# Moving the softmax division, the mode scalings and some loads within the rows of a shifted-window attention and Fourier block

## The chip, the core and the metric

The kernel runs on one core of a Trainium2 chip. A core has five engines, each with its own instruction list, worked off in order: TensorE (PE, matrix products; PEld is its loading of weights), VectorE (DVE), ScalarE (ACT), GpSimd (POOL) and SyncE (SP), which here only issues DMAs. The engines synchronise by semaphores. The metric is the time of one execution on the device in microseconds (us); the figure of a kernel is the median of its runs.

## The reference

The input x is 32 images of 56 x 56 positions with 128 channels, all in float32. Two residual layers follow each other:

```python
x = x + attention(_gn(x), rpb_table, w_qkv, w_proj, b_proj)
x = x + fourier(_gn(x), w0, w1, W1, b1, W2, b2)

# attention: roll by 3, windows of 7 x 7, four heads of 32 channels
qkv  = win @ w_qkv.T
attn = softmax(q * hd**-0.5 @ k.T + bias + mask)
out  = (attn @ v) @ w_proj.T + b_proj          # rolled back

# fourier: DCT along one axis, 32 modes mixed per mode, inverse DCT
x_fty = dct(x, axis=-1)                         # and the same along the other axis
out_y = einsum('bixy,ioy->boxy', x_fty[..., :32], w0)
h     = idct(out_x) + idct(out_y)
b     = relu(h @ W1 + b1) @ W2 + b2
```

`_gn` is a group normalisation over 32 groups of four channels, with mean and variance taken over a whole image.

## The kernel before

**Rows and cycles.** An image is cut into eight rows of eight windows, 256 rows in all. The main loop runs over cycles, and cycle r starts the attention of row r. One row passes through several cycles: in its own, queries and keys (`attn_qk`), scores (`attn_scores`), row maximum and its subtraction (`attn_max`: VectorE L496, GpSimd L497), exponential (`attn_exp`, ScalarE L503) and values (`attn_v`, L456, copied by ScalarE L463); in the next, the sum and its reciprocal (VectorE, L508 and L510) and the division (`attn_divide`, six GpSimd operations at L522 that also write the blocks in the form in which they are transposed); two cycles on, the transpose (`attn_transpose`, L532); three on, probabilities times values (`attn_values`, L547, evicted by ScalarE L579 and VectorE L577), the projection (`attn_project`, L592, with the residual added at L600 and stored to the DRAM tensor `scr`); four on, the sums and squares (`attn_sums`, `attn_squares`) from which the second normalisation is made.

**The Fourier layer.** It runs beside the attention of the following images, from cycle `CONV_BEGIN` = 11 on. With c counted from the cycle in which an image's Fourier part begins: c = 0 is the statistics (`fourier_stats`, a generator worked off in steps) and the transform along the width (`transform`, L699, transposed by VectorE L715 in `turn_modes`); c = 1 and 2 the transform along the height; c = 3 to 5 the mixing of the modes (`mix`, L747); c = 5 to 8 the inverse (`modes_back`, L786, fetched at L804 and L809); c = 8 to 15 without 11 the feed-forward part in seven groups (`ff_in`, `ff_out`, both by the helper `halved`, L113; the result is added at L865). Between transform and mixing, ScalarE scales the modes by the image's reciprocal deviation (`scale_modes`, L722, two operations for each half) and shifts the first mode (`shift_modes`, L727). Since c = 0 falls on the fourth row of an image, row i of the attention stands beside a fixed c: row 3 beside 0 and 8, row 5 beside 2 and 10, row 6 beside 3, row 0 beside 5 and 13.

**The next image.** It is loaded in four quarters (`load_quarter`, four DMAs each, one buffer `xin` after the first image) and transposed by VectorE (`turn_quarter`, L334 to L339); then statistics of its rows (`row_stats`, L356) and its normalisation in four steps (`image_norm`, called by `norm_step`) follow. `next_steps` says in which row each quarter and each row's statistics come.

**Order.** The order on TensorE, ScalarE, VectorE and GpSimd is the order of the program text: cycles before 11 are written out in `first_rows`, later ones are put together from `halves_first`, `eighths`, `quarters`, `behind_max` and `halves_last`. SyncE's order is left to the scheduler of the kernel's framework. A DMA that overwrites a tile waits for what wrote or read it before: `mix_weights` first sets one column of its tile with GpSimd, so that the load is not issued before GpSimd has come that far in its list.

**Buffers.** Scores lie in two buffers; up to row 8 there is a third, in `y_of[1]`, which the Fourier part uses later (`attn_buffer`). The attention takes its PSUM banks from four in rotation (`attn_bank`), the Fourier part from four others (`conv_bank`).

Of the kernel before, what the change touches and what calls it, by code (L numbers as in the profile page):

```python
# [14 lines left out]
P = 128  # L15
# [32 lines left out]
def swin_fourier_kernel(  # L48
# [212 lines left out]
    def mix_weights(k):  # L261
        dst, src = ((w1sb, w1), (w0sb, w0))[k // 4]
        m = slice(k % 4 * NM // 4, (k % 4 + 1) * NM // 4)
        nc.gpsimd.memset(dst[:, m.start, :1], 0.0)
        nc.sync.dma_start(dst[:, m], src[:, m])
# [33 lines left out]
    def attn_buffer(r):  # L299
        return a_sb[r % 3 if r < CONV_BEGIN - 2 else r % 2]  # L300
# [234 lines left out]
    def attn_values(im, i, r):  # L535
# [3 lines left out]
        po = [attn_bank(), attn_bank()]  # L539
# [104 lines left out]
    def fourier_stats(im):  # L644
        pg = attn_bank()

        for k, t in enumerate((im.tot, im.part[:, (NWR - 1) % 4])):
            t = t.rearrange("p k g -> p (k g)")
            for hs in HALVES:
                nc.tensor.matmul(  # L650
                    pg[hs, : C // 2], lhsT=gmean, rhs=t, start=(k == 0), stop=(k == 1)
                )
        own = small.tile([P, 2, C // 4], F32, tag="own", name="own", bufs=1)
        nc.vector.scalar_tensor_tensor(
            out=own,
            in0=pg[:, : C // 2].rearrange("p (k g) -> p k g", k=2),
            scalar=4.0,
            in1=gavg.unsqueeze(1).to_broadcast([P, 2, C // 4]),
            op0=ALU.mult,
            op1=ALU.mult,  # L660
        )
        ms = small.tile([P, 2], F32, tag="ms", name="ms")
        nc.vector.tensor_reduce(ms, own, axis=AX.X, op=ALU.add)
        nm2 = small.tile([P, 1], F32, tag="nm2", name="nm2")
        nc.vector.scalar_tensor_tensor(
            out=nm2, in0=ms[:, 0:1], scalar=-1.0, in1=ms[:, 0:1], op0=ALU.mult, op1=ALU.mult
        )
        ve = small.tile([P, 1], F32, tag="ve1", name="ve1")
        nc.vector.scalar_tensor_tensor(
            out=ve, in0=nm2, scalar=1e-5, in1=ms[:, 1:2], op0=ALU.add, op1=ALU.add  # L670
        )
        rstd = small.tile([P, 1], F32, tag="rstd1", name="rstd1")
        nc.gpsimd.tensor_tensor(rstd, ve, mhalf, ALU.pow)
        im.rstd = rstd
        yield
        shift = small.tile([P, 1], F32, tag="shift", name="shift")
        nc.vector.scalar_tensor_tensor(
            out=shift, in0=ms[:, 0:1], scalar=-SQRT_S, in1=rstd, op0=ALU.mult, op1=ALU.mult
        )
        im.shift = shift  # L680
        yield
# [36 lines left out]
    def scale_modes(im, width, h):  # L718

        y = y_of[width][:, : NM * S].rearrange("p (k h n r) -> p h r n k", k=NM, h=2, r=2)[:, h]  # L720
        for r, t in enumerate(im.modes.pop((width, h))):
            nc.scalar.mul(y[:, r], t.rearrange("p (n k) -> p n k", k=NM), im.rstd)  # L722
# [226 lines left out]
    def halves_first(cycle):  # L949
        begins = [im for im, c in fourier(cycle) if c == 0]  # L950
        last, j = row(cycle - 4)
        tokens_bias(cycle)
        divide(cycle)
# [11 lines left out]
        if cycle % NWR == 0:  # L965
            norm_step(cycle)
        if cycle % NWR == NWR - 1:
            norm_step(cycle)
# [23 lines left out]
    def half_columns(cycle, rest=False):  # L992
        for im, c in fourier(cycle):
            if rest and c != 3:
                continue
            if c == 0:
                next(im.stats, None)
            elif c == 3:
# [22 lines left out]
    def eighths(cycle):  # L1021
# [3 lines left out]
        for im, c in fourier(cycle):  # L1025
            if c == 0:
                for h in range(2):
                    transform(im, True, h)
                    turn_modes(im, True, h)
            if c in (1, 2):  # L1030
# [15 lines left out]
    def first_scale(cycle):  # L1046
        for im, c in fourier(cycle):
            if c == 0:
                shift_modes(im, True)
            elif c in (1, 2):  # L1050
                scale_modes(im, False, c - 1)
                if c == 2:
                    shift_modes(im, False)

    def width_scale(cycle):
        for im, c in fourier(cycle):
            if c == 0:
                for h in range(2):
                    scale_modes(im, True, h)
# [9 lines left out]
    def next_steps(cycle):  # L1069
        b, i = divmod(cycle, NWR)  # L1070
        steps = {
            int(b == 0): ((0, 0), ()),
            1 + int(b == 0): ((0, 1), ()),
            4: ((1, 0), (0, 1, 2)),
            5: ((1, 1), (3, 4, 5)),
            6: (None, (6, 7)),
        }
        return (b + 1, *steps.get(i, (None, ()))) if b + 1 < NB else (b + 1, None, ())

    def next_quarter(cycle):  # L1080
        b, quarter, _ = next_steps(cycle)
        if quarter:
            turn_quarter(images[b], *quarter)

    def wrap_rows(cycle):
        b, _, _ = next_steps(cycle)
# [3 lines left out]
    def next_groups(cycle):  # L1090
        b, _, rows = next_steps(cycle)
# [7 lines left out]

    def halves_last(cycle):  # L1100
# [3 lines left out]
        width_scale(cycle)  # L1104
# [9 lines left out]
        first_scale(cycle)  # L1114
# [5 lines left out]
    def next_begin(cycle):  # L1120
        b, quarter, _ = next_steps(cycle + 1)
# [7 lines left out]
    def first_rows(cycle):  # L1129
        im, i = row(cycle)  # L1130
        im3, i3 = row(cycle - 3)
        if im:
            attn_qk(im, i)
        if cycle:
# [4 lines left out]
        if im:  # L1139
            attn_scores(im, i, cycle)  # L1140
            attn_max(cycle)
        divide(cycle)
# [3 lines left out]
        for _ in range(cycle in (0, NWR - 1, NWR)):  # L1146
            norm_step(cycle)
        last, j = row(cycle - 4)
        if last:
            attn_sums(last, j)  # L1150
            attn_squares(last, j)
            add_sums(last, j)
# [7 lines left out]
        next_quarter(cycle)  # L1160
# [18 lines left out]
    with tc.manual_schedule(engines={ET.PE, ET.Activation, ET.DVE, ET.Pool}):  # L1179
# [13 lines left out]
        extra = y_of[1][:, : NH * NP * WT].rearrange("p (t w j) -> p t w j", t=NH, w=NP)  # L1193
        a_sb.append(extra)
        for cycle in range(NB * NWR + CONV_BEGIN + FF_AT[-1] - NWR + 1):
# [4 lines left out]
            if not row(cycle - 3)[0]:  # L1200
# [3 lines left out]
                width_scale(cycle)  # L1204
                half_columns(cycle)
                half_columns(cycle, True)
                first_scale(cycle)
# [79 lines left out]
```

## Time and profile before

| | us |
|---|---|
| median of three runs | 3293.78 |
| lowest and highest run | 3292.73, 3294.27 |
| the profiled execution, its own time | 3297.98 |
| its span, first to last instruction | 3296.2 |
| mean granted TensorE clock (share of full speed) | 0.991 |
| VectorE, ScalarE, GpSimd busy | 2605.2, 2057.4, 2335.7 |
| largest group on GpSimd: division L522, 1518 operations | 1289.4 |
| largest group on ScalarE: L830, 896 operations | 499.4 |
| idle of GpSimd before L522, waiting for the reciprocal L510 | 263.0 |

The profile is of one execution. An operation is named by its line, its engine and its tiles, output first: `y<-modes,rstd` writes y from modes and rstd. An idle time is put down to what ended it last, as `<-ENGINE tile line`. Engines other than the limiting one may idle at no cost. Times within the span are counted from its first instruction. TensorE's matmuls overlap, so that two of them in a row start closer together than one lasts.

### The profile page before, as it was taken

The page shows a single profiled execution, that of the slowest core. Times are in us where ns is not written, and L with a number is a line of the kernel's source. Part 1 is how long each engine was busy: PE and PEld are TensorE (multiplying, and loading weights), DVE is VectorE, ACT ScalarE, POOL GpSimd, SP SyncE. Part 2 cuts the span into 40 slices and gives each one's busy share as a digit, 9 for nine tenths or more (in the row PEclk, how much of TensorE's full clock was granted, in tenths as well). Part 3 has the DMA queues.
Part 4 walks back from the last instruction along what each step waited for, and adds up shares of the span by engine and source line. Part 5 has one row for each costly group of instructions (what it writes and reads, how often), then busy time and mean ns, then how long its engine had stood idle before and what let it go on. Part 6 is the DMA issues. An engine that isn't in the chain of part 4 may idle for free.

```text
span 3296.2 us, 151336 instructions
## 1 busy us (share of the span) xinstructions
PE 3170.4 (96%) x65408; PEld 2394.9 (73%) x65408; DVE 2605.2 (79%) x5098; ACT 2057.4 (62%) x3680; POOL 2335.7 (71%) x2610
## 2 busy tenths in 40 slices
PE   4689999999999999999999999999999999999999
PEld 3467777777777777777777777777777777777776
DVE  7888888887888878888888888877888887888751
ACT  3456666666666666666666666666666666666663
POOL 7777777777777777777777777777777777777741
PEclk9799999999999999999999999999999999999999
DMA  6555555555555555555555555555555655555453
GB/s 105 116 124 142 140 138 142 133 146 140 137 140 135 136 145 138 138 142 138 139 144 143 136 142 138 136 142 143 137 139 136 143 139 139 138 143 135 121 140 96
DMA packets 1168160, 448.40 MB, mean 136 GB/s; under 512 B 520107, under 2 KB 1137629, under 8 KB 1167493
## 3 DMA queue, kind: packets, MB, share of 16 engines
q1 hardware_dynamic: 1159300, 437.38, 54.9%
q8 instruction: 514, 8.42, 1.1%
q10 hardware_dynamic: 7584, 1.18, 0.3%
q14 instruction: 154, 1.25, 0.1%
q0 software_dynamic: 608, 0.17, 0.0%
HBM read 276.97 MB, written 161.48 MB: 133 GB/s over the span
## 4 chain that ended last, share of the span: by engine, by line
PE 76%; ACT 10%; DVE 7%; POOL 3%; DMA 2%; issue 2%; SPq 1%; ACTq 0%; POOLq 0%; DVEq 0%
PE pc L113 35%; PE pa L113 9%; PE pa L456 7%; PE pc L747 5%; PE pc L786 5%; PE pa L592 5%; PE pa L478 4%; PE pa L547 4%; ACT k L443 2%; PE pc L699 2%; ACT hid L830 2%; ACT y L722 2%; POOL a L497 2%; DVE modes L715 1%; DVE a L486 1%
## 5 line engine op out<-in xcount | busy, mean ns | idle before, releaser
L522 POOL TENSOR_TENSOR blocks<-a,rs 128x512 f32<-128x512 f32 x1518 | 1289.4, 856 | 483.9 <-DVE rs L510 263.0
L113 PE MATMUL pc<-wff,hid 128*64 128x128 f32 x12544 | 742.0, 273 | 1.3 <-ACT hid L830 1.0
L113 PE MATMUL pc<-xf,wff 128*64 128x512 f32 (+2 forms) x3584 | 718.9, 539 | 1.1 <-DVE xf L804 0.9
L113 PEld LDWEIGHTS pc<-wff,hid 128*64 128x64 f32 x12544 | 706.5, 137 | 11.1 <-ACT hid L830 5.3
L497 POOL TENSOR_TENSOR a<-a,mx 128x784 f32<-128x784 f32 x253 | 381.4, 1508 | 314.9 <-DVE mx L496 281.6
L113 PEld LDWEIGHTS pc<-xf,wff 128*64 128x64 f32 x3584 | 280.6, 136 | 354.9 <-issue 239.9
L830 ACT ACTIVATE hid<-pc,b1sb 128x512 f32<-128x512 f32 (+2 forms) x896 | 499.4, 643 | 42.7 <-PE pc L113 42.7
L463 ACT COPY v<-pa 128x512 f32<-128x512 f32 x256 | 151.9, 593 | 482.8 <-PE pa L456 482.7
L113 PE MATMUL pa<-xw,wn 128*64 128x392 f32 x2048 | 400.4, 501 | 31.3 <-ACT wn L412 28.8
L865 DVE TENSOR_TENSOR res<-pc,res 128x512 f32<-128x512 f32 (+3 forms) x257 | 142.9, 567 | 319.4 <-issue 173.2
L503 ACT ACTIVATE a<-a 128x784 f32<-128x784 f32 x253 | 217.3, 859 | 281.4 <-POOL a L497 281.4
L486 DVE TENSOR_TENSOR a<-pa,bm 128x392 f32<-128x392 f32 x506 | 261.1, 557 | 84.8 <-PE pa L478 70.6
L837 POOL TENSOR_TENSOR res<-res,b2sb 128x512 f32<-128x512 f32 (+2 forms) x256 | 265.3, 1042 | 87.4 <-DMA res<-scr 78.4
L443 ACT ACTIVATE k<-pa,bqkv,heads 128x392 f32<-128x392 f32 x512 | 318.1, 673 | 8.0 <-PE pa L113 0.9
L532 DVE STREAM_TRANSPOSE eT<-blocks 128x1024 f32<-128x1024 f32 x256 | 313.6, 1225 | 2.4 <-POOL blocks L522 2.4
L127 POOL TENSOR_TENSOR xr<-xr,bproj 128x384 f32<-128x384 f32 (+1 forms) x256 | 292.8, 1144 | 25.6 <-DMA xr<-in_x_dram 17.1
L456 PE MATMUL pa<-wn,xw 128*64 128x128 f32 x4096 | 289.5, 283 | 8.6 <-issue 2.5
L547 PEld LDWEIGHTS pa<-eT,v 49*32 49x32 f32 x16384 | 173.6, 106 | 154.3 <-ACT hid L830 48.7
L592 PE MATMUL pa<-wproj,oT 128*64 128x128 f32 x3584 | 251.8, 276 | 19.6 <-DVE oT L577 17.4
L508 DVE TENSOR_REDUCE sm<-a 128x16 f32<-128x784 f32 x253 | 243.0, 961 | 23.9 <-ACT a L503 23.8
L456 PEld LDWEIGHTS pa<-wn,xw 128*64 128x64 f32 x4096 | 225.5, 139 | 48.5 <-ACT oT L579 16.9
L722 ACT ACTIVATE y<-modes,rstd 128x448 f32<-128x448 f32 x256 | 252.0, 1122 | 4.4 <-DVE modes L715 4.4
(110 smaller groups left out, 4908.3 us busy)
## 6 DMA issues: line engine op xcount, KB each, us to landing
zscr<-z SPq DMA_DIRECT2D x512, 112.0 KB
xin<-in_x_dram SPq DMA_DIRECT2D x496, 112.0 KB
htok<-scr SPq DMA_DIRECT2D x256, 196.0 KB
zT<-zscr SPq DMA_DIRECT2D x192, 256.0 KB
res<-scr SPq DMA_DIRECT2D x160, 256.0 KB
out_dram<-res SPq DMA_DIRECT2D x160, 256.0 KB
scr<-x SPq DMA_DIRECT2D x256, 112.0 KB
xr<-in_x_dram SPq DMA_DIRECT2D x256, 84.0 KB
```

The lines of the kernel that those rows point to most:

```text
L113: nc.tensor.matmul(dst[ps], lhsT=lhsT[:, ps], rhs=rhs, start=start, stop=stop)
L127: nc.gpsimd.tensor_tensor(piece, piece, bproj.unsqueeze(1).to_broadcast([P, n, C]), ALU.add)
L443: nc.scalar.activation(k_sb[:, u], pk[:, :RT].rearrange("p (w j) -> p w j", j=WT), AF.Identity, bias=im.bias[:, 3 + u : 4 + u], scale=head ...
L456: nc.tensor.matmul(pv[HALVES[w % 2], w // 2 * C : (w // 2 + 1) * C], lhsT=im.half[i // NP][:, t0 : t0 + JP], rhs=im.w[:, 2 * C : 3 * C], s ...
L486: nc.vector.tensor_tensor(a[:, 2 * hp : 2 * hp + 2, :, 0:WT].rearrange("p u w j -> p w u j"), ps[hp][:, :RT].rearrange("p (w u j) -> p w u ...
L497: nc.gpsimd.tensor_tensor(a3, a3, mx.unsqueeze(2).to_broadcast([P, 2 * NWR, WT]), ALU.subtract)
L522: nc.gpsimd.tensor_tensor(dst[to, k, :, :n], a3[src, :, kb * KB : kb * KB + n], rs[src].unsqueeze(2).to_broadcast([src.stop - src.start, 2 ...
L532: nc.vector.transpose(eT.rearrange("p t (k j) -> p k t j", k=2), blocks[r % 2])
L547: nc.tensor.matmul(po4[u][h * HD : (h + 1) * HD, pr], lhsT=v[ks, pr, h * HD : (h + 1) * HD], rhs=eT[ks, h * NP + pr, :WT], start=True, sto ...
L592: nc.tensor.matmul(pp[hs, (n - n0) * C : (n - n0 + 1) * C], lhsT=oT[:, t0 : t0 + JP], rhs=wproj, start=True, stop=True,)
L722: nc.scalar.mul(y[:, r], t.rearrange("p (n k) -> p n k", k=NM), im.rstd)
L830: nc.scalar.activation(hf[:, :n], ph[:, :n], AF.Relu, bias=b1sb[:, f : f + 1])
```

## The change

It has these parts, all of them in the order or place of work; the arithmetic is the same but for two small operations of the second statistics.

- **Division.** In rows 0, 3, 4, 5 and 7 of each image (`EARLY`) the sum, the reciprocal and the division of a row come at the end of its own cycle, behind the exponential and ahead of `last_out` and `attn_project`. In rows 1, 2 and 6 they stay at the start of the next.
- **Mode scalings.** Of the two scalings of a height half (c = 1, 2) one comes before the exponential and one behind it. Of the width modes, the first half is scaled before the exponential at c = 0, the second and the shift in c = 1, behind the eviction of the outputs. Before, all four stood ahead of the exponential at c = 0.
- **Second statistics.** The step that ends in the reciprocal deviation is moved behind the width transform's transposes. One VectorE operation and one on GpSimd (`tensor_scalar`) replace two on VectorE.
- **First normalisation.** The first of its steps in row 7 moves to the start of the cycle.
- **Quarters.** Both quarters of the first half are transposed in row 0: the second is loaded when the first has been transposed, and transposed behind the maximum of the same row. Statistics of rows 0 to 3 come in row 1, of 4 and 5 in row 5.
- **Output banks.** The two PSUM banks of `attn_values` change places: VectorE evicts the one that is taken first again.
- **First rows.** Sums, squares and their adding up come before the division, the fourth normalisation step of the second image right behind its queries and keys, and its quarters early in the cycle from cycle 8 on. The mixing weights are loaded by ScalarE's queue, without GpSimd's setting of a column.
- **Third score buffer.** It is used for rows below 15, not 9, and lies in a buffer of the tag `xf`.

```diff
 def mix_weights(k):
-    nc.gpsimd.memset(dst[:, m.start, :1], 0.0)
-    nc.sync.dma_start(dst[:, m], src[:, m])
+    nc.scalar.dma_start(dst[:, m], src[:, m])
...
-    return a_sb[r % 3 if r < CONV_BEGIN - 2 else r % 2]
+    return a_sb[r % 3 if r < CONV_BEGIN + 4 else r % 2]
...
-    po = [attn_bank(), attn_bank()]
+    po = [attn_bank(), attn_bank()][::-1]
...
     nc.vector.tensor_reduce(ms, own, axis=AX.X, op=ALU.add)
-    (nm2 and ve: two nc.vector.scalar_tensor_tensor)
+    yield
+    nc.vector.scalar_tensor_tensor(out=nvar, in0=ms[:, 0:1], scalar=ms[:, 0:1],
+        in1=ms[:, 1:2], op0=ALU.mult, op1=ALU.subtract)
+    nc.gpsimd.tensor_scalar(ve, nvar, -1.0, 1e-5, ALU.mult, ALU.add)
...
 def halves_first(cycle):
+    if cycle % NWR == NWR - 1:
+        norm_step(cycle)
     tokens_bias(cycle)
-    divide(cycle)
+    if cycle == CONV_BEGIN or (cycle - 1) % NWR not in EARLY:
+        divide(cycle)
...
 def eighths(cycle):
             for h in range(2):
                 transform(im, True, h)
                 turn_modes(im, True, h)
+            next(im.stats)
+        if c == 1:
+            for r in range(2):
+                scale_modes(im, True, 1, r)
+            shift_modes(im, True)
...
-def first_scale(cycle):
+def scale_first(cycle, r):
+        if c == 0 and r == 0:
+            for k in range(2):
+                scale_modes(im, True, 0, k)
         elif c in (1, 2):
-            scale_modes(im, False, c - 1)
-            if c == 2:
+            scale_modes(im, False, c - 1, r)
+            if (c, r) == (2, 1):
                 shift_modes(im, False)
...
 def next_quarter(cycle):
     if quarter:
         turn_quarter(images[b], *quarter)
+    if late:
+        xins[(b, *late)] = load_quarter(b, *late)
...
 def next_groups(cycle):
+    if late:
+        turn_quarter(images[b], *late)
...
+EARLY = (0, 3, 4, 5, 7)
 def halves_last(cycle):
-    width_scale(cycle)
+    scale_first(cycle, 0)
...
         attn_exp(cycle)
-    first_scale(cycle)
+    scale_first(cycle, 1)
+    if row(cycle)[0] and cycle % NWR in EARLY:
+        divide(cycle + 1)
     last_out(cycle)
     attn_project(im, j)
...
 def first_rows(cycle):
         attn_qk(im, i)
+    if cycle == NWR:
+        norm_step(cycle)
+    if last:
+        attn_sums(last, j)
+    if cycle >= NWR:
+        next_quarter(cycle)
...
         attn_max(cycle)
+    if last:
+        attn_squares(last, j)
+        add_sums(last, j)
     divide(cycle)
```

## The prediction

> **What bounds the kernel.** I read the page first: busy shares, then the slices.
>
> ```profile
> PE 3170.4 (96%) x65408; PEld 2394.9 (73%) x65408; DVE 2605.2 (79%) x5098; ACT 2057.4 (62%) x3680; POOL 2335.7 (71%) x2610
> ...
> PE   4689999999999999999999999999999999999999
> ...
> PEclk9799999999999999999999999999999999999999
> ```
>
> TensorE is busy all the time except in the first three slices of 82 us. Added up over stretches of 50 us, it idles 86 us in the first 300 us (24 of them before its first matmul, which the change leaves alone) and about 1.2% afterwards. So there are two stages with different limits: a start, rows 0 to some 18, where GpSimd and VectorE set the pace, and a steady state of some 29 images in which only TensorE counts. There each image repeats 2044 matmuls in one order and takes 98.55 to 100.4 us, mean 99.15.
>
> Next, the waits of TensorE between 292 and 3190 us (in total, times, longest), and the one row of the waits of all engines that repeats per image:
>
> ```profile
> PE pc L747 <- ACT y L727: 14.8, 29, 1.7
> PE pc L786 <- issue: 6.5, 11, 1.1
> ```
>
> ```profile
> PEld pa L456 <- ACT oT L579: 16.9, 58, 0.3
> ```
>
> Hardly anything else is waited for. The issue waits move by nine matmuls from image to image and have no releaser; the change does not touch them. The other two are 29 and 2 x 29 times: once and twice per image. The timeline of one row 5 to 6 shows both (start, duration, engine, what):
>
> ```profile
> 1545.39 1.17 DVE L715 STREAM_TRANSPOSE modes<-pc 128x448 f32<-128x448 f32 x2
> 1545.62 1.50 POOL L497 TENSOR_TENSOR a<-a,mx 128x784 f32<-128x784 f32 x1 [1.37 <-DVE mx L496]
> ...
> 1547.15 0.86 ACT L503 ACTIVATE a<-a 128x784 f32<-128x784 f32 x1 [2.10 <-POOL a L497]
> ...
> 1547.91 2.03 ACT L722 ACTIVATE y<-modes,rstd 128x448 f32<-128x448 f32 x2
> ...
> 1548.39 1.50 PE L113 MATMUL pa<-xw,wn 128*64 128x392 f32 x8
> ...
> 1549.98 0.34 ACT L727 ACTIVATE y<-y,shift 128x56 f32<-128x56 f32 x1
> ...
> 1550.37 1.97 PE L747 MATMUL pc<-w1sb,y 128*64 128x128 f32 x32 [0.47 <-ACT y L727]
> ...
> 1553.01 0.91 PE L478 MATMUL pa<-k,q 64*64 64x98 f32 x32
> ...
> 1553.17 0.66 DVE L577 TENSOR_SCALAR oT<-pa,bqkv 128x147 f32<-128x147 f32 x3
> ...
> 1553.50 0.47 ACT L579 ACTIVATE oT<-pa,bqkv 128x196 f32<-128x196 f32 x1
> ...
> 1554.02 1.09 PE L456 MATMUL pa<-wn,xw 128*64 128x128 f32 x16
> ```
>
> **Mode scalings.** Before the exponential ScalarE idles 2.10 us; behind it stand both scalings (2.03) and the shift (0.34), and the height mix waits for the shift. From the first query-key matmul (1548.39) to the mix is 1.98 us; the same eight matmuls take 1.33 in rows 3 and 4. That is 0.65 lost, and the mix block then takes 1.90 instead of 1.75: 0.8 per image. The change puts one scaling before the exponential. Its transpose is ready near 1546.0, so it runs 1546.0 to 1547.1; the exponential still starts when GpSimd releases it, near 1547.15; one scaling and the shift end near 1549.4. The mix could start at 1549.72, so the wait goes, with 0.3 us in hand. In the rows of the width modes two scalings and the shift move to row 4 behind the output eviction, where ScalarE idles 2.4 us before the values' copy at 1531.8 and needs 1.12 + 0.93 + 0.34 = 2.4: it just fits, and that copy has no early reader. **Gain 29 x 0.8 = 23 us.**
>
> **Reversed output banks.** The values' matmuls (L456) reuse the first of the two output banks. ScalarE evicts it at 1553.97 after two z copies; the matmuls start 0.05 later, 1.01 after the scores instead of 0.73. Reversed, they wait for VectorE's three evictions, which end at 1553.83: gain 0.14. In row 7 both end together, at 1564.1, because the norm's first step stands before VectorE's evictions; the change moves that step to the row's start, VectorE ends some 0.2 earlier: gain 0.2. Elsewhere the values start over 0.5 us behind either. **29 x 0.34 = 10 us** of the 17 to 19 that the wait costs.
>
> **Divisions at the row's end.** Sum and reciprocal (0.96 + 0.25 us) now stand before the residual adds L865 and L600 on VectorE, behind the exponential. Queued behind them are these two adds; the next row's output matmuls (L547) wait for L600's bank. Row by row, with exponentials' ends from the trace: row 0 has VectorE idle anyway (below); row 3's exponential comes two scalings earlier; row 4's L600 ends near 1537.9 instead of 1537.6, needed at 1540.8; row 5's near 1551.1, needed at 1551.6 with TensorE already earlier (the tightest, 0.5 us); row 7's near 1572.9, needed at 1576.2. All hidden, cost 0. GpSimd's division starts 1 to 2 us earlier, but its reader, the transpose, comes two rows later: gain 0 in the steady state. Removed, per image, is one 0.16 us operation of VectorE; a small one is added on GpSimd, which the trace lacks: between 0.1 (its 128x1 memset) and 0.55 (its 128x1 power). I take 0.3, hidden in front of scalings that start later.
>
> **Statistics in row 3, and a rule.** L665 and L669 stood before the output evictions and took 0.16 us at the least, but L665 0.88 in most images. The Trainium skill, SBUF — State Buffer, "Who interferes with whom", says that a VectorE instruction with two SBUF inputs and a GpSimd one that reads SBUF exclude each other for a whole instruction; GpSimd is dividing there, so the trace agrees. Counting durations alone, the evictions and the four mode transposes start earlier and TensorE's inverse transform (2.1 us there, 1.26 for the same 48 matmuls in row 1) gets its banks 0.35 earlier: 10 us. By the rule the replacing operation, also with two SBUF inputs, meets the division's last pieces, right before the score adds and L804, for which the next output bank waits. I take little: 0.1 per image, **2 us**, bounds 0 and 10.
>
> **Quarters in one row.** In row 0 the second quarter is loaded when the first is turned and turned in the same row.
>
> ```profile
> 1579.83 1.24 DVE L532 STREAM_TRANSPOSE eT<-blocks 128x1024 f32<-128x1024 f32 x1
> ...
> 1585.73 0.69 DVE L865 TENSOR_TENSOR res<-pc,res 128x512 f32<-128x512 f32 x1 [4.67 <-issue]
> ```
>
> VectorE's gap of 4.67 holds turning (1.11 + 0.89) and sum with reciprocal (1.21) if the data are there by about 1582.5. The first quarter is turned by 1575.1; four issues of 0.5 us and the 3.3 to 4.9 us that such loads took to land in the chain of waits at the start give 1580.5 to 1582. So hidden. From a landing at 1586.5 on (1591.2, when the next output matmuls are due, less 2.0 + 1.25 + 1.4 + 0.1), TensorE waits.
>
> **The start.** GpSimd's list there runs almost without a gap, 8.7 us per row; its gaps are what can be won:
>
> ```profile
> 140.09 1.50 POOL L497 TENSOR_TENSOR a<-a,mx 128x784 f32<-128x784 f32 x1 [4.93 <-DVE mx L496]
> ...
> 154.29 5.35 POOL L522 TENSOR_TENSOR blocks<-a,rs 128x512 f32<-128x512 f32 x6 [2.50 <-DVE rs L510]
> ```
>
> The 4.93 arise because VectorE waited 4.30 for the second statistic's power behind a division; the shift now comes after the row's maximum, and sums come before divisions: about -4. Early divisions shorten 2.50 and its likes (1.08, 2.09): -3. Two waits for xr, 3.27 and 3.12 near 97 and 109 us, come from SyncE's queue: 24 small transform constants hold it for 7 to 8 us twice. Moving the mixing weights to ScalarE's queue: the Trainium skill, Trainium Kernel Development and Optimization, "Key Constraints", says that all queues share the same 16 DMA engines and only issue time is saved: by the rule 8 x 0.36 = 3 us of issue. The rows show more, some 21 us in which SyncE stood waiting for the memsets before these loads; but of what GpSimd waits for, the constants remain, so I take -1. Against it: in row 8 both quarters stand early in VectorE's list, and before, half of the first was issued at 98.0, landing near 102, where VectorE would want it at 95. That costs 0 to 8; I take 4. The third score buffer removes one wait of 2.85, inside the xr wait: 0. **Sum -4**, bounds -12 and +4.
>
> **Sum.** 23 + 10 + 2 + 4 = 39 us. The profiled execution took 3297.98 (span 3296.2): it becomes 3259. The median of the runs, 3293.78, lies 4.2 lower: **3255 us**.
>
> **Rivals.** (a) *The wait moves on*: the mix then waits for GpSimd's subtraction or the values for VectorE, and half of the steady gain is kept, nothing at the start: 18 us, 3276. For it: 0.3 and 0.14 us in hand are thin. Against: ScalarE's idle 2.10 is real. (b) *Slower*: the late quarter. SyncE issued this very quarter at 1575.7, 1577.3, 1579.1 and 1583.6, between other loads; kept so, it lands at 1586.9 to 1588.5, past 1586.5. Each us beyond costs 29. It decides against the change from 1.3 us per image (39 / 29), a landing at 1587.8; at 1589 it is 2.5 x 29 - 39 = +34, 3328. Against: the loads are now asked for early in the row, ahead of those that parted them. (c) *More*: the start gains 12 and row 3 its 10: 23 + 10 + 10 + 12 = 55, 3239. (d) The change does nothing to TensorE, since it was busy 96% anyway: refuted by the two waits, small chance.
>
> **Chances.** Forecast 0.57, (a) 0.18, (c) 0.17, (b) 0.05, (d) 0.03. The measurement can tell some 0.2%, 6.6 us, from no change. Faster 0.92; same 0.03; slower 0.05. Range 3236 to 3279: from a little beyond (c) to a little beyond (a); the forecast's own part is 3246 to 3266.
>
> **What would show it.** Right: the wait of L747 for L727 gone, L456 no more waiting for ScalarE's oT, mean image near 98 us, GpSimd's gap before 140 us gone. Wrong: waits of L547 for L600 in row 1 or 6, or VectorE's L334 waiting for xin once per image.

## The result and the profile after

| | before | after |
|---|---|---|
| median of seven runs each, us | 3294.27 | 3282.72 |
| lowest and highest run, us | 3291.82, 3296.53 | 3281.83, 3287.67 |
| span of the profiled execution, us | 3296.2 | 3280.9 |
| granted TensorE clock | 0.991 | 0.991 |

The ratio is 0.9968, with a 95% interval from 0.9956 to 0.9979. By the medians the change is 11.5 us faster; the forecast was 39, and rival (a) stood for 3276. The time lies 3.7 us above the predicted range.

First the page of the changed kernel: TensorE has lost 15.6 us of busy time, and nothing in the shares tells what was won and what was missed.

```profile
PE 3154.8 (96%) x65408; PEld 2394.1 (73%) x65408; DVE 2637.5 (80%) x5066; ACT 2100.4 (64%) x3680; POOL 2346.8 (72%) x2634
```

Next the two longest waits of TensorE's matmuls between 292 and 3180 us (in total, times, longest), and then of its weight loads the wait for the eviction oT:

```profile
PE pa L455 <- ACT oT L578: 14.8, 28, 0.6
PE pc L789 <- issue: 7.7, 12, 1.2
```

```profile
PEld pa L455 <- ACT oT L578: 27.8, 57, 0.8
```

The mix no longer waits for ScalarE. (L747, L727, L456 and L579 of before are L750, L730, L455 and L578 now.) But the values, which should have stopped waiting for ScalarE's eviction oT, wait for it more than before: 14.8 us now stand in the matmuls' own list, and the weight loads' share has grown from 16.9 to 27.8.

The steady state can be laid side by side matmul by matmul, since each image repeats the same 2044. Means over 28 images, in us from the start of one block of matmuls to the start of the next:

| block | before | after | difference |
|---|---|---|---|
| row 6, query-key matmuls up to the mix | 2.02 | 1.33 | -0.68 |
| row 6, the mix block | 1.90 | 1.85 | -0.05 |
| row 3, inverse transform | 2.03 | 1.61 | -0.42 |
| row 3, values behind it | 0.92 | 1.05 | +0.13 |
| row 7, scores up to the values | 0.99 | 1.43 | **+0.44** |
| whole image | 99.14 | 98.60 | -0.53 |

The scalings' 0.73 and row 3's 0.29, less the 0.44 of row 7, are 0.58 per image; the whole image shows 0.53. 28 x 0.53 is 14.9 us. The steady state begins 0.85 us later than before (in row 24, the first of the fourth image, the matmuls on its mean start at 282.20 instead of 281.35), and the end is 0.8 shorter. So the gain in span is the steady state's, and the start gave nothing.

How row 6 looks now is shown by ScalarE's timeline (start, duration), in which L502 is the exponential of row 5, and by TensorE's:

```profile
1538.19 1.17 ACT L725 ACTIVATE y<-modes,rstd 128x448 f32<-128x448 f32 x1 [1.01 <-DVE modes L718]
1539.21 0.86 ACT L502 ACTIVATE a<-a 128x784 f32<-128x784 f32 x1
1539.97 1.14 ACT L725 ACTIVATE y<-modes,rstd 128x448 f32<-128x448 f32 x1
1541.15 0.34 ACT L730 ACTIVATE y<-y,shift 128x56 f32<-128x56 f32 x1
```

```profile
1540.52 1.50 PE L113 MATMUL pa<-xw,wn 128*64 128x392 f32 x8
1541.85 1.92 PE L750 MATMUL pc<-w1sb,y 128*64 128x128 f32 x32
```

One scaling lies ahead of the exponential L502, one behind it, and the shift ends at 1541.49, 0.36 us before the mix wants it (0.3 was foreseen). Row 7 is where the time went back. ScalarE and TensorE there, from the exponential of row 6 on:

```profile
1550.24 0.86 ACT L502 ACTIVATE a<-a 128x784 f32<-128x784 f32 x1 [1.36 <-POOL a L496]
1551.01 0.57 ACT L432 ACTIVATE q<-pa,bqkv 128x392 f32<-128x392 f32 x1
1551.48 1.24 ACT L442 ACTIVATE k<-pa,bqkv,heads 128x392 f32<-128x392 f32 x2
1552.60 0.73 ACT L628 ACTIVATE xr<-x,valid 128x512 f32<-128x512 f32 x1
1553.22 2.42 ACT L833 ACTIVATE hid<-pc,b1sb 128x512 f32<-128x512 f32 x4
1555.50 0.47 ACT L578 ACTIVATE oT<-pa,bqkv 128x196 f32<-128x196 f32 x1
```

```profile
1553.82 0.81 PE L546 MATMUL pa<-eT,v 49*32 49x49 f32 x64
1554.56 0.90 PE L477 MATMUL pa<-k,q 64*64 64x98 f32 x32
1556.02 0.54 PE L455 MATMUL pa<-wn,xw 128*64 128x128 f32 x5 [0.56 <-ACT oT L578]
```

From the exponential on, ScalarE's list has no gap: exponential, q, k, xr, four hid, and last the eviction oT, which ends at 1555.97. The probabilities whose product it evicts were done on TensorE by 1554.63, so the eviction is late because of the list ahead of it, and that list starts when GpSimd's subtraction (L496) is done. TensorE may come to this place as early as it likes: the values start 0.05 us after that eviction. Before the change the same place looked like this, with 0.06 us from eviction to values:

```profile
1563.64 0.47 ACT L579 ACTIVATE oT<-pa,bqkv 128x196 f32<-128x196 f32 x1
```

```profile
1563.17 0.91 PE L478 MATMUL pa<-k,q 64*64 64x98 f32 x32
1564.17 1.09 PE L456 MATMUL pa<-wn,xw 128*64 128x128 f32 x16
```

What releases the subtraction is seen in GpSimd's list, before and after. Row 6's subtraction stands behind row 5's division (`blocks`), and that waits until row 5's exponential and sum are done:

```profile
1548.60 1.28 POOL L127 TENSOR_TENSOR xr<-xr,bproj 128x512 f32<-128x512 f32 x1
1551.43 5.35 POOL L522 TENSOR_TENSOR blocks<-a,rs 128x512 f32<-128x512 f32 x6 [1.55 <-ACT k L443]
1556.86 1.50 POOL L497 TENSOR_TENSOR a<-a,mx 128x784 f32<-128x784 f32 x1
```

```profile
1542.03 5.35 POOL L521 TENSOR_TENSOR blocks<-a,rs 128x512 f32<-128x512 f32 x6 [1.33 <-ACT q L432]
1547.45 1.29 POOL L127 TENSOR_TENSOR xr<-xr,bproj 128x512 f32<-128x512 f32 x1
1548.71 1.50 POOL L496 TENSOR_TENSOR a<-a,mx 128x784 f32<-128x784 f32 x1
```

Before, the bias of the next tokens (`xr`, 1.28 us) filled idle time ahead of the division; now it stands between division and subtraction.

A last look at the start. VectorE's timeline in row 8, and GpSimd's near 140 us:

```profile
101.46 1.09 DVE L333 STREAM_TRANSPOSE xw<-xin 128x512 f32<-128x512 f32 x1 [6.90 <-DMA xr<-in_x_dram]
...
111.74 1.11 DVE L333 STREAM_TRANSPOSE xw<-xin 128x512 f32<-128x512 f32 x1 [2.77 <-DMA xin<-in_x_dram]
```

```profile
139.84 1.50 POOL L496 TENSOR_TENSOR a_extra<-a_extra,mx 128x784 f32<-128x784 f32 x1
143.99 5.36 POOL L521 TENSOR_TENSOR blocks<-a_extra,rs 128x512 f32<-128x512 f32 x6 [2.65 <-DVE rs L509]
```

The gap of 4.93 before L496 is gone, as foreseen. The one before L521 is not (2.50 before, 2.65 now), and VectorE stands 9.7 us waiting before it turns the second image's quarters, where it stood 0.7 before.

### The profile page after: what moved, and what is told of

Read it like the earlier page. It is cut to its first block, busy times and chain, and to the rows that moved or that the text cites. A ratio compares the mean times of both kernels' runs of the same rounds, so it can differ in the third digit from the quotient of the medians.

```text
span 3280.9 us, 151050 instructions
## 1 busy us (share of the span) xinstructions
PE 3154.8 (96%) x65408; PEld 2394.1 (73%) x65408; DVE 2637.5 (80%) x5066; ACT 2100.4 (64%) x3680; POOL 2346.8 (72%) x2634
## 4 chain that ended last, share of the span: by engine, by line
PE 83%; ACT 7%; DVE 3%; DMA 2%; issue 2%; SPq 2%; POOL 0%; ACTq 0%; DVEq 0%; POOLq 0%
PE pc L113 38%; PE pa L113 10%; PE pa L455 7%; PE pc L789 5%; PE pa L591 5%; PE pc L750 5%; PE pa L477 5%; PE pa L546 4%; PE pc L702 3%; ACT hid L833 2%; ACT k L442 2%; SPq L760 1%; ACT xr L628 1%; ACT z L758 1%; DMA zscr<-z 1%
## 5 line engine op out<-in xcount | busy, mean ns | idle before, releaser
L521 POOL TENSOR_TENSOR blocks<-a,rs 128x512 f32<-128x512 f32 x1506 | 1280.5, 857 | 399.2 <-DVE rs L509 251.2
L496 POOL TENSOR_TENSOR a<-a,mx 128x784 f32<-128x784 f32 x251 | 377.7, 1505 | 358.6 <-DVE mx L495 341.6
L442 ACT ACTIVATE k<-pa,bqkv,heads 128x392 f32<-128x392 f32 x512 | 319.0, 674 | 14.9 <-PE pa L113 1.1
L725 ACT ACTIVATE y<-modes,rstd 128x448 f32<-128x448 f32 x256 | 276.3, 1137 | 71.5 <-DVE modes L718 64.0
L502 ACT ACTIVATE a<-a 128x784 f32<-128x784 f32 x251 | 214.9, 856 | 151.1 <-POOL a L496 150.9
L455 PE MATMUL pa<-wn,xw 128*64 128x128 f32 x4096 | 289.1, 283 | 22.0 <-ACT oT L578 16.4
L127 POOL TENSOR_TENSOR xr<-xr,bproj 128x384 f32<-128x384 f32 (+1 forms) x256 | 292.6, 1143 | 20.6 <-DMA xr<-in_x_dram 7.9
L432 ACT ACTIVATE q<-pa,bqkv 128x392 f32<-128x392 f32 x256 | 149.3, 583 | 220.7 <-PE pa L113 219.0
L576 DVE TENSOR_SCALAR oT<-pa,bqkv 128x147 f32<-128x147 f32 (+2 forms) x768 | 171.5, 279 | 140.5 <-PE pa L546 138.3
```

The costliest lines, as they stand in the source:

```text
L127: nc.gpsimd.tensor_tensor(piece, piece, bproj.unsqueeze(1).to_broadcast([P, n, C]), ALU.add)
L442: nc.scalar.activation(k_sb[:, u], pk[:, :RT].rearrange("p (w j) -> p w j", j=WT), AF.Identity, bias=im.bias[:, 3 + u : 4 + u], scale=head ...
L455: nc.tensor.matmul(pv[HALVES[w % 2], w // 2 * C : (w // 2 + 1) * C], lhsT=im.half[i // NP][:, t0 : t0 + JP], rhs=im.w[:, 2 * C : 3 * C], s ...
L496: nc.gpsimd.tensor_tensor(a3, a3, mx.unsqueeze(2).to_broadcast([P, 2 * NWR, WT]), ALU.subtract)
L521: nc.gpsimd.tensor_tensor(dst[to, k, :, :n], a3[src, :, kb * KB : kb * KB + n], rs[src].unsqueeze(2).to_broadcast([src.stop - src.start, 2 ...
```

## The experiments

Each kernel was timed against the kernel before on the same chip. Ratios are to it. Two things bound what a single profile can tell: runs of the before kernel had medians from 3294.3 to 3296.9, and the waits called "issue" wander by about 0.1 us per image from one kernel to another.

### One part alone, on the kernel before

**Mode scalings only (b_scale).** `scale_modes`, `scale_first`, its two calls and the lines for c = 1 in `eighths`, as in the diff, and nothing else. The calls:

```diff
-    width_scale(cycle)
+    scale_first(cycle, 0)
...
         attn_exp(cycle)
-    first_scale(cycle)
+    scale_first(cycle, 1)
```

> The kernel before with the mode scalings alone spread as in the change. Theory (the wait of the height mix for ScalarE's shift was worth 0.65 us and 0.15 us of the block behind it, per image): TensorE's wait of L747 for the shift is gone, the mean image takes 0.7 us less, 21 us in all, some 3273 us where the kernel before takes 3294. Rival (ScalarE's freed time is lost again at the next wait in the same image): less than 8 us are gained. The GpSimd queue is as before, so the scores to values stretch of row 7 should stay at 0.99 us.

Measured: 3295.14 us, ratio 0.9998 (0.9989 to 1.0007): nothing. Row 6's mix wait is gone (-0.68 and -0.05), and row 7's stretch from scores to values went from 0.99 to 1.74. TensorE's waits between 292 and 3190 us name it:

```profile
PE pa L456 <- ACT oT L579: 23.7, 29, 0.8
```

The whole 0.73 us per image is handed on to row 7. TensorE comes there earlier and finds the eviction even a little later: the scaling that now stands ahead of row 5's exponential delays that by 0.23 us (medians, counted from row 5's queries), and with it row 5's division, row 6's subtraction and, by 0.24, row 7's eviction. This part, forecast at 23 us, is worth nothing alone.

**Early divisions only (b_early).**

```diff
-    divide(cycle)
+    if cycle == CONV_BEGIN or (cycle - 1) % NWR not in EARLY:
+        divide(cycle)
...
+    if row(cycle)[0] and cycle % NWR in EARLY:
+        divide(cycle + 1)
```

> The kernel before with the divisions of rows 0, 3, 4, 5 and 7 alone moved to the row's end. Theory (GpSimd then does the bias of the tokens after the division instead of in its idle time ahead of it, so row 6's subtraction and exponential and all of ScalarE's list into row 7 come later): the stretch from row 7's scores to its values grows from 0.99 to some 1.4 us, 12 us in all, some 3306 us. Rival (the stretch grew because of the norm's step or the scalings): it stays at 0.99 and the time at 3294 within 4.

Measured: 3304.42 us, ratio 1.0025 (1.0015 to 1.0036): 7.9 us slower. Row 7's stretch grew by 0.28. The prediction had looked for what the sum and reciprocal push back on VectorE, and not at GpSimd's own list, where the next row's bias (`tokens_bias`, L127) now stands behind the division instead of ahead of it. Row 5's division starts 0.98 us earlier, but the bias behind it takes 1.3, so row 6's subtraction starts 0.27 us later; everything in ScalarE's list above comes 0.27 later with it.

**Second statistics only (b_stats).**

```diff
+    yield
+    nc.vector.scalar_tensor_tensor(out=nvar, in0=ms[:, 0:1], scalar=ms[:, 0:1],
+        in1=ms[:, 1:2], op0=ALU.mult, op1=ALU.subtract)
+    nc.gpsimd.tensor_scalar(ve, nvar, -1.0, 1e-5, ALU.mult, ALU.add)
...
     turn_modes(im, True, h)
+    next(im.stats)
```

(the two VectorE operations that these replace, and the step's old call at c = 0, are taken out)

> The kernel before with the move of the second statistics alone: the step that ends in the reciprocal deviation behind the width transform's transposes, with one operation on VectorE and one on GpSimd in place of two on VectorE. Theory (what the changed kernel gains in row 3 is this move): the inverse transform's stretch in row 3 falls from 2.03 to about 1.6 us, what follows gives 0.1 back, the row-7 wait is untouched because the gain lies ahead of the chain that sets it or is eaten by it there; time lower by 28 x 0.3 = 8 us, or by nothing if row 7 takes it back. Rival (the gain in row 3 comes from the divisions or scalings moved): the stretch stays near 2.0 and the time within 0.1% of before.

Measured: 3285.61 us, ratio 0.9972 (0.996 to 0.9983), 8.7 us. Row 3's inverse transform takes 1.62 (2.03 before), the values behind it 0.13 more: 0.28 per image, as much as the changed kernel's gain in row 3. The steady state also begins 2.5 us earlier, in cycle 12 where the gap of 4.93 was.

**Evicting engines exchanged (b_swap).** The one-piece bank goes to VectorE, the one of three pieces to ScalarE:

```diff
-    if u:
+    if not u:
         nc.vector.tensor_scalar(d, f, im.bias[:, 2:3], None, ALU.add)
     else:
         nc.scalar.activation(d, f, AF.Identity, bias=im.bias[:, 2:3])
```

> The kernel before with the evicting engines of the attention outputs exchanged, nothing else. Theory (this is what the reversal of the banks was taken to do: the values' matmuls wait for VectorE instead of ScalarE): the stretches from scores to values in rows 5 and 7 fall from 0.98 to about 0.83 each, 28 x 0.3 = 8 to 9 us, to 3285; the prediction's 10 us for the banks was then the right size for the wrong edit. Rival (VectorE's eviction in row 7 ends as late as ScalarE's, 27.05 against 27.06 us behind row 5's queries, because the norm's first step stands ahead of it): only row 5 gains, 4 us, or the wait turns up at VectorE, 0.

Measured: 3282.70 us, ratio 0.9958 (0.9945 to 0.997). The values gain 0.18 in row 6, which the expectation calls row 5, and 0.07 in row 7; row 3 is 0.17 shorter too, and the steady state begins 3.6 us earlier (the cause of these two was not looked for). This one-line exchange alone thus takes about as much off the kernel before as the whole change did.

**Scalings and exchange together (b_scale_swap).** Both edits above.

> The kernel before with the mode scalings spread and the evicting engines exchanged. The scalings alone brought nothing, since row 7's wait for ScalarE's eviction grew by the 0.74 us that row 6 gave. Theory (the mode scalings are worth their 0.73 us per image as soon as row 7 does not wait for ScalarE): row 6's mix stays at 1.33 and row 7's stretch at about 0.85, time 28 x (0.73 + 0.3) = 29 us below before, to 3265. Rival (the chain from GpSimd's subtraction over the exponential to both engines' evictions sets row 7, whichever engine is waited for): row 7's stretch comes to about 1.4 with VectorE named as the releaser, the time 8 to 12 us below before.

Measured: 3278.23 us, ratio 0.9949 (0.9937 to 0.9962). Against the exchange alone the mix again gives 0.69 and row 7 takes back 0.68; now it is VectorE's eviction that the values wait for. The rival is right in the releaser that it names. VectorE's timeline shows why, and TensorE's what it costs:

```profile
1551.58 0.36 DVE L380 BATCH_NORM_AGGREGATE stat<-st 128x2 f32<-128x48 f32 x1
1551.97 0.21 DVE L383 STREAM_TRANSPOSE turned<-stat 128x32 f32<-128x32 f32 x1
1552.22 0.18 DVE L369 TENSOR_REDUCE gsums<-turned 128x8 f32<-128x32 f32 x1
1552.44 0.56 DVE L372 TENSOR_SCALAR gmeans<-gsums 128x32 f32<-128x32 f32 x1
1552.92 0.41 DVE L577 TENSOR_SCALAR oT<-pa,bqkv 128x196 f32<-128x196 f32 x1
```

```profile
1551.77 0.91 PE L478 MATMUL pa<-k,q 64*64 64x98 f32 x32
1553.38 0.33 PE L456 MATMUL pa<-wn,xw 128*64 128x128 f32 x2 [0.71 <-DVE oT L577]
```

The four operations ahead of the eviction are the first normalisation's step, which the change moves to the start of row 7 and this kernel leaves where it was.

### The changed kernel with one part altered

**Banks in the old order (a_unrev).**

```diff
-    po = [attn_bank(), attn_bank()][::-1]
+    po = [attn_bank(), attn_bank()]
```

> The changed kernel with the two output banks in their old order. Prediction's step (the reversal makes the values wait for VectorE's eviction instead of ScalarE's, 0.34 us per image): 10 us slower than the changed kernel, 3293. Rival (the bank that the values take is the one that is evicted by ScalarE whichever is taken first): 3283 within 3, and the values still wait for ScalarE's oT in row 7.

Measured: 3285.72 us, ratio 0.9972 (0.996 to 0.9984), not to be told from the change's 0.9968. None of the blocks tabled above differs by more than 0.05 us; a mean image is 0.15 us longer, of which 0.11 are waits called "issue". By the semaphores in the traces the first of the values' matmuls waits for ScalarE in 244 of 256 rows, with the reversal, without it, and in the kernel before. With the engines exchanged it waits for VectorE alone in 182. So the values take the one-piece bank in either order of allocation, and the reversal does nothing that can be measured. Why the allocation falls so was not settled.

**Bias ahead of each early division (a_bias_first).**

```diff
     if row(cycle)[0] and cycle % NWR in EARLY:
+        tokens_bias(cycle + 1)
         divide(cycle + 1)
```

(and `tokens_bias` left out at the next cycle's start where it was done here)

> The changed kernel, with the bias of the next row's tokens put ahead of each division at the row's end. Theory as for b_early: row 7's stretch from scores to values goes back from 1.43 to about 1.0 us, 12 us in all, and the start gains some 1.2 us in each of three rows, 4 us: 3267 us where the changed kernel takes 3283. Rival (the wait in row 7 comes from another cause): 3283 within 4.

Measured: 3268.88 us, ratio 0.9918 (0.9903 to 0.9933). Row 7's stretch falls from 1.43 to 0.83, a mean image from 98.60 to 98.13. GpSimd's subtraction in row 6 ends 1.14 us earlier, and ScalarE's eviction in row 7 comes 0.87 earlier with it. GpSimd's list there shows the division directly behind the bias, and a subtraction that now waits for VectorE's maximum instead:

```profile
1535.13 1.27 POOL L127 TENSOR_TENSOR xr<-xr,bproj 128x512 f32<-128x512 f32 x1
1536.43 5.35 POOL L521 TENSOR_TENSOR blocks<-a,rs 128x512 f32<-128x512 f32 x6
1541.97 1.51 POOL L496 TENSOR_TENSOR a<-a,mx 128x784 f32<-128x784 f32 x1 [0.19 <-DVE mx L495]
```

The part of the expectation that spoke of the start is a miss, the steady state begins no earlier.

**Engines exchanged (a_swap).** The edit of b_swap, on the changed kernel.

> The changed kernel with the evicting engines of the attention outputs exchanged: VectorE evicts the bank that is one piece, ScalarE the one of three pieces. In the changed kernel the values' first matmul of row 7 waits for ScalarE's one piece, which stands behind the row's exponential. Theory (it is the place of that one eviction in ScalarE's list that costs 0.44 us per image): the values then wait for VectorE, whose eviction in row 7 ends about 0.6 us earlier, the stretch from row 7's scores to its values falls from 1.43 to about 0.85, and the time falls by 28 x 0.55 = 15 us, to 3267. Rival (both engines hang on the same chain from GpSimd's subtraction over the exponential to queries and keys, and ScalarE's three pieces then come later still, which the projection waits for): the stretch falls but the wait turns up behind it, the time within 5 us of the changed kernel's.

Measured: 3262.55 us, ratio 0.9905 (0.989 to 0.992), about 20 us below the change. A mean image takes 97.87: row 7 gives 0.59, row 6 0.14. VectorE and ScalarE in row 7:

```profile
1544.13 0.42 DVE L576 TENSOR_SCALAR oT<-pa,bqkv 128x196 f32<-128x196 f32 x1 [0.47 <-PE pa L546]
```

```profile
1542.83 2.43 ACT L833 ACTIVATE hid<-pc,b1sb 128x512 f32<-128x512 f32 x4
1545.11 0.77 ACT L578 ACTIVATE oT<-pa,bqkv 128x147 f32<-128x147 f32 x3
```

VectorE now evicts as soon as the product is there (its wait is for TensorE), and TensorE's values start at 1544.87 with no wait. ScalarE's eviction ends as late as ever, at 1545.88, and no one waits for it.

**Exchange, divisions all late (a_swap_late).** `EARLY = ()`.

> The changed kernel with the engines exchanged and all divisions at the start of the next row, as before the change. Theory (an early division serves a reader two rows later, and its only effect on TensorE was the later bias, which the exchange hides): the mean image within 0.1 us of the same kernel with early divisions, 97.87, the start up to 3 us later, time 3260 to 3267. Rival (late divisions push GpSimd's subtraction or VectorE's evictions back and a wait reappears): mean image 98.2 or more, 3271 or more.

Measured: 3264.52 us, ratio 0.9902 (0.9888 to 0.9915), against 0.9905 with early divisions; a mean image 98.00 against 97.87, which is the size of the issue waits. Once the values do not hang on ScalarE, the early divisions neither gain nor cost anything that can be measured.

**Second image's quarters as before (a_row8).** The loads and turnings of its first half again at the ends of cycles 8 and 9, the statistics of rows 0 to 3 in cycle 11 (four lines in `next_steps`, not shown):

```diff
-    if cycle >= NWR:
-        next_quarter(cycle)
...
-    if cycle < NWR:
-        next_quarter(cycle)
+    next_quarter(cycle)
```

> The changed kernel with the second image's quarters again where they stood before the change: turned at the end of cycles 8 and 9 instead of early in cycle 8, the statistics of rows 0 to 3 in cycle 11. Theory (the early turning in row 8 is what keeps the start from gaining): the two waits of VectorE for the loaded quarter, 6.90 and 2.77 us in row 8, go, the cycles 9 to 12 start up to 9.7 us earlier, the first steady image starts 4 to 9 us earlier and the time falls by as much, to 3274 to 3279. Rival (GpSimd and TensorE make the delay up by cycle 12 anyway, and what the start lacks lies in GpSimd's waits for the reciprocal): the waits go, the first steady image starts within 1.5 us of where it did, the time stays within 0.1% of the changed kernel's.

Measured: 3277.49 us, ratio 0.9949 (0.9936 to 0.9961); the interval overlaps the change's.

**The same on top of the exchange (a_swap_row8).**

> The changed kernel with the engines exchanged and the second image's quarters as before, without the bias edit: the combination of three edits less one. Theory (with the engines exchanged row 7 no longer hangs on the chain that the bias edit shortens): the same as the combination of three, 3256 to 3260. Rival (the bias edit gives something of its own): 3262 or more.

Measured: 3261.12 us, ratio 0.9892 (0.9877 to 0.9907). The two pairs are read together. Here is when each cycle starts (ScalarE's eviction of its queries), in us later than in the kernel before:

| cycle | change | a_row8 | a_swap | a_swap_row8 |
|---|---|---|---|---|
| 8 | 0.30 | 0.90 | -2.32 | -0.58 |
| 9 | 10.71 | 0.92 | 6.93 | -0.24 |
| 10 | 8.94 | 0.62 | 5.80 | -0.73 |
| 12 | -0.16 | -5.21 | -2.79 | -3.32 |
| 19 | 1.28 | -3.95 | -2.03 | -2.34 |
| 24 | 0.85 | -3.03 | -1.75 | -2.05 |

The early turning holds cycle 9 up by some 7 to 10 us. Most of it is made up by cycle 12: the gap in which GpSimd had waited before is gone, and the work held up is done instead (read from the trace, not tried alone). What is left is 3.9 us at cycle 24 in the one pair and 0.3 in the other. Between 0 and 4 us is all that can be said.

**All three edits (a_best).** Bias first, exchange and quarters as before, on the changed kernel.

> The changed kernel with three edits: the bias of the next row ahead of each early division, the evicting engines exchanged, and the second image's quarters in cycles 8 and 9 as before the change. Theory (three separate losses, two of them in row 7): the row-7 stretch falls to about 0.75, a mean image to about 98.0 us, the start gives 4 to 9 us: 3260 to 3266. Rival (the bias alone has already taken row 7's wait away, and the start makes up its own delay): no better than the bias edit alone, 3266 to 3271.

Measured: 3257.85 us (3257.19 to 3258.79), ratio 0.9889 (0.9875 to 0.9902): faster than both kernels. A mean image is 97.89, like the exchange alone, and without the bias edit the ratio was 0.9892, so the bias adds nothing of its own once the engines are exchanged. The exchange is the edit that counts.

### One table for row 7

Medians over 27 images, in us from the start of ScalarE's eviction of row 5's queries:

| kernel | scores of row 7 begin | ScalarE's oT ends | VectorE's oT ends | values begin |
|---|---|---|---|---|
| before | 26.12 | 27.06 | 27.06 | 27.11 |
| b_scale | 25.61 | **27.30** | 27.30 | 27.36 |
| b_early | 26.13 | **27.34** | 27.35 | 27.40 |
| b_scale_swap | 25.47 | 27.58 | **27.04** | 27.09 |
| after | 25.61 | **27.02** | 26.42 | 27.07 |
| a_bias_first | 25.61 | 26.15 | 26.42 | 26.45 |
| a_swap | 25.46 | 27.31 | 25.98 | 26.30 |

Where a wait remains, the values begin 0.05 to 0.06 us after the eviction in bold; in the last two rows they follow the scores by 0.84, the least in any kernel here. Before, b_scale_swap and after begin within 0.04 of each other, however early the scores are: a second chain, over row 5's division, row 6's subtraction and ScalarE's or VectorE's list, sets the place. The change loosens it at VectorE (26.42), where nobody waits. In the changed kernel the wait can be removed in two ways: the exchange makes the values wait at VectorE, and the bias ahead of the division loosens the chain at ScalarE (26.15).

## Why the prediction was wrong

- **Mode scalings: the mechanism right, the gain not kept.** "Gain 29 x 0.8 = 23 us" was nearly right for row 6 (0.73 measured: 0.68 for the wait and 0.05 for the block behind it, where 0.65 and 0.15 had been put). What failed is the step that asks what is late next. The 0.3 us in hand were weighed for the mix itself, and the next place on TensorE that another engine sets was not followed with TensorE 0.8 us earlier. That place is row 7, whose values already waited for the eviction (0.99 us behind the scores, where 0.83 is the least). There 0.44 of the 0.73 went in the change, and in b_scale all of it. So of the 23 us some 8 were kept: 28 x 0.29.
- **Reversed banks: this step was wrong, and the largest term hung on the same wait.** "Reversed, they wait for VectorE's three evictions" is what the program text suggests and not what the kernel does (a_unrev): 0 instead of 10 us. The two terms were added as if they were independent; they are not. With the edit that does what the reversal was taken to do (a_swap), a mean image is 99.14 - 97.87 = 1.27 us shorter than before, and the forecast's steady state was (23 + 10 + 2) / 29 = 1.21. That the two are so close is in part luck: row 3 gives 0.22 of the 1.27 where 0.07 was taken, and the rest of the image, scalings and banks, 1.05 where 1.14 was. Nor is this the only step that would have saved the steady state: a_bias_first leaves the banks as they are and has a mean image of 98.13, 1.01 shorter than before. Row 7's wait in the changed kernel stood on two steps, this one and the divisions' below, and mending either removes it.
- **Norm step moved.** "VectorE ends some 0.2 earlier" was 0.64 (27.06 to 26.42), and useless while the values waited for ScalarE; with the exchange it is what sets b_scale_swap (27.04) apart from a_swap (25.98), as far as two kernels that differ in more than this step can show it.
- **Divisions early: "All hidden, cost 0".** Right only once the exchange is made (a_swap_late). Alone they cost 7.9 us, since the bias came to stand behind the division on GpSimd: an operation queued behind the moved one, on the engine that was not looked at. "Gain 0 in the steady state" fails too. It asked only for the division's reader two rows later, and not for what stands behind the division in the same list: with the bias ahead of it (a_bias_first), row 6's subtraction and all that hangs on it come over 1 us earlier.
- **Statistics in row 3: 0.1 taken, 0.28 measured** (b_stats): 8 us where 2 were taken, near the bound of 10. The rule on shared SBUF access (the Trainium skill, SBUF — State Buffer, "Who interferes with whom") made the prediction fear that the replacing operation would again be shut out by GpSimd, and the traces show that it is. In the kernel before, L665 started inside one of the division's pieces 27 times of 32; each time it ended 0.02 us after that piece did, so that it took what was left of the piece, 0.29 to 0.89 us. The other five took 0.16. In the changed kernel the new L665 still starts inside a piece 24 times, and in 23 of them ends 0.01 to 0.02 us after it. But no more than 0.3 us of the piece is left there, and it takes 0.18 to 0.31, where it takes 0.17 to 0.18 outside. So the meeting that was feared took place; its price, a few hundredths of a us where the old one mostly paid 0.7, was what the prediction had wrong. GpSimd's replacing operation takes 0.19, within the bounds of 0.1 and 0.55. The lines of L665 before and after (shortest, median and longest in ns):

```profile
L665 DVE SCALAR_TENSOR_TENSOR nm<-ms x32: 159/874/890, 129.6 to 3186.1; 128x1 f32<-128x1 f32 x32
```

```profile
L665 DVE SCALAR_TENSOR_TENSOR nm<-ms x32: 174/226/310, 135.0 to 3173.9; 128x1 f32<-128x1 f32 x32
```

- **Start: -4 forecast, none measured** (the steady state begins 0.85 later). The early turning was foreseen where it happened (landing at 102, wanted at 95; measured 101.46 and 94.56, though the profile names another load, xr, as what ended the wait), and a second wait of 2.77 was not; its lasting cost, between 0 and 4, is at or under the 4 taken. The early divisions' -3 did not come: alone (b_early) they brought the steady state forward by 0.6. By the trace, exponential, sum and reciprocal lie between subtraction and division, and GpSimd has little else to do meanwhile. The mixing weights' queue and the third score buffer were not tried alone.
- **Quarters in row 0: hidden, as forecast.** VectorE's timeline shows the second quarter turned without a wait, and the add L868 waiting for TensorE and not the reverse:

```profile
1572.84 1.10 DVE L333 STREAM_TRANSPOSE xw<-xin 128x512 f32<-128x512 f32 x1
1573.97 0.90 DVE L338 STREAM_TRANSPOSE xw<-xin 128x384 f32<-128x384 f32 x1
...
1577.59 0.69 DVE L868 TENSOR_TENSOR res<-pc,res 128x512 f32<-128x512 f32 x1 [0.92 <-PE pc L113]
```

  This row begins 8.15 us earlier than in the profile before (ScalarE's eviction of its queries starts at 1563.98 instead of 1572.13), so 1572.84 here is 1580.99 there. By then the load was there, as reckoned (1580.5 to 1582), and 5.5 us ahead of the 1586.5 from which TensorE would wait. In 9 of 27 images VectorE did wait for this quarter, 1.13 us at the most, but TensorE never, and rival (b) did not come about.

Rival (a), "the wait moves on", is what happened, at a third place: neither the mix for GpSimd nor the values for VectorE, but the values for ScalarE still. It kept 15 us in the steady state where (a) said 18; the prediction had given (a) a chance of 0.18.

## What to carry to other kernels

A wait removed on the busiest engine is worth only what the next place keeps where another engine sets the time: shift that engine's timeline earlier by the gain and check every later row of the period, not the next block alone. Two edits that bear on one chain are priced together, since each may be worth nothing without the other. Before a gain is put on a change of buffer order, see in the waits which buffer is in truth taken, and in whose list the operation that frees it stands. When an operation is moved, look at what is queued behind it on its own engine, and not only at who reads its result.

## What was not expected of the hardware

The same one-piece eviction (128x196) takes 0.42 us on VectorE and 0.47 on ScalarE, and the three pieces of the other half 0.67 and 0.77 together: so it was the place in the list rather than the engine's speed that was worth 20 us. A VectorE operation on one element per partition took anything from 0.16 to 0.89 us, and its length told how much was left of the GpSimd operation inside which it had started: it ended 0.02 us after that, 27 times of 27.
